# Causal attention with a routed feed-forward on one Trainium2 core: part of the softmax sums on ScalarE, the rest in one buffer on GpSimd

## The chip, the cores and the metric

The kernel runs on one core of a Trainium2 chip. The metric is the device time of one execution in microseconds: lower is better. Three runs of the kernel before stand beside one execution that was taken with the hardware profiler.

## The reference

Two sequences of 2048 positions with 512 features pass through one pre-norm block: attention with 16 heads of 32, rotary positions and a causal mask, then a feed-forward in which two of eight low-rank experts are chosen per position. All of it is fp32.

```python
x = x + attn(layernorm(x))
x = x + ffn(layernorm(x))

# attn: q, k, v = x @ Wq.T, x @ Wk.T, x @ Wv.T, split in 16 heads; q, k = rope(q), rope(k)
scores = einsum('bhqd,bhkd->bhqk', q, k) / sqrt(32)
attn = softmax(where(causal, scores, -inf))
return einsum('bhqk,bhkd->bhqd', attn, v) @ Wo.T      # heads put side by side again

# ffn: base layer, gate of two experts, low-rank update
result = x @ base_w.T + base_b
gate = top-2 of softmax(x @ router_w.T + router_b), made to add to 1
mid = einsum('nd,edr->ner', x, lora_A) * gate
return result + 2 * einsum('ner,erd->nd', mid, lora_B)
```

## The kernel before

**Blocks, steps and beats.** The 4096 positions are cut into eight blocks of 512 (`blocks`, four per sequence, j = 0 to 3 within a sequence). The 16 heads are taken four at a time, as the four 32-row quarters of a 128-row tile. So there are 32 steps (n, g): block n, group of heads g. A step needs its queries against the keys of all blocks up to its own: 4(j+1) key tiles of 128.

Every step has two passes over its scores, and the first pass of one step runs beside the second pass of the step before (`side_by_side`).

- `row_maxima`: the scores with queries in rows (`sm`, L367). VectorE takes the largest of each row into `pm`, with the causal mask on the diagonal block (L375) and without it elsewhere (L380). `split` writes the negated maxima as three bfloat16 parts into `parts`; `turned` transposes them (L397) into `max` (L401).
- `attend`: the scores with keys in rows (`sc`, L463). Two small bfloat16 matmuls per pair (`shift`, L471) add the negated maxima, ScalarE takes the exponential (`weigh`, L485) into a tile `pt` of four heads, GpSimd zeroes what lies above the diagonal (L494), and `weighted` multiplies the weights with the values into the bank `av` (L519).

In the inner loop of `side_by_side` two heads of the maxima go beside the other two of the weights; a tile of 128 keys or queries takes two such passes. `phase` counts them.

**Sums.** The softmax's denominators come out of the same weights. When two neighbouring key tiles have been weighted, GpSimd adds the second `pt` to the first (L534), and three phases later `summed` multiplies the sum with a column block of ones into the bank `den` (L545): one group of four matmuls for every two key tiles. After the last, the sums leave through DRAM to be spread over the partitions (`sums`, `few`), VectorE takes reciprocals, they come back (`over`, `sum`), and GpSimd multiplies `ctx` with them (L581).

**Other work.** `prepare` normalises and transposes the next block (`xnps_a`, L155) and projects keys, queries and values (L185, L210); `finish` makes the output projection (`ops`, L239), the router and the experts (`mid`, L265), and the base layer (`yps`, L320) of the block before, and stores it. They come as stages with a cost and a due phase in the list `waiting`; after every pass the main loop does what its running `credit` allows, and what is urgent.

**Order.** TensorE, ScalarE and VectorE run in the order in which the program is written (`manual_schedule`). The tile framework orders GpSimd and the DMA queue of SyncE itself. `between` runs what stands in `due`, the delayed `weighted` and `summed`; when a pass got nothing else, `ahead` may run a `summed` one phase early. `before` runs the `due` entries whose `pt` tile is about to be taken again, of which there are `PTS = 4`.

**Banks.** PSUM has eight banks. Six are handed out in turn by `bank` to scores, projections and transposes; `av` and `den` have one each.

```python
def bank(name, shape=(P, BLK), dtype=F32):
    banks[0] += 1
    return ps.tile(list(shape), dtype, tag=f"ps{banks[0] % 6}", name=name)
```

All weights are loaded once, at the start, and stay in SBUF.

Of the kernel before, what the change touches and what calls it, by code (L numbers as in the profile page):

```python
# [15 lines left out]
P = 128  # L16
# [13 lines left out]
PTS = 4  # L30
# [4 lines left out]
def preln_attention_moe_lora(  # L35
# [34 lines left out]
    def bank(name, shape=(P, BLK), dtype=F32):  # L70
        banks[0] += 1
        return ps.tile(list(shape), dtype, tag=f"ps{banks[0] % 6}", name=name)
# [54 lines left out]
    wo = load_weight(wo_t, "wo")  # L127
# [3 lines left out]
    base_w = load_weight(base_wt, "base_w")  # L131
    exp_out = const.tile([ER, D], F32, name="exp_out")
    nc.sync.dma_start(out=exp_out, in_=expert_out)

# [23 lines left out]
    def prepare(n):  # L158
# [23 lines left out]
        def project(which, w, g):  # L182
            pj = bank(f"{which}ps_{n}_{g}")
            for c in range(NC):
                nc.tensor.matmul(  # L185
                    out=pj,
                    lhsT=w[:, c, bass.ts(g, P)],
                    rhs=held["xn_t"][:, c, :],
                    start=(c == 0),
                    stop=(c == NC - 1),  # L190
                )
            if which == "k":
                dest = kv.tile([P, BLK], F32, tag="k", name=f"k_{n}_{g}")
            else:
                dest = wide.tile([P, BLK], F32, tag="q", bufs=3, name=f"q_{n}_{g}")
            made[which].append(dest)
            sw = p2.tile([P, BLK], F32, tag="tmp", bufs=5, name=f"sw_{which}_{n}_{g}")
            nc.vector.stream_shuffle(sw, pj, SWAP)  # L198
            nc.vector.tensor_mul(dest, pj, held["turn"][0])
            nc.gpsimd.tensor_mul(sw, sw, held["turn"][1])  # L200
            nc.gpsimd.tensor_add(dest, dest, sw)  # L201
# [25 lines left out]
    def finish(n, ctx_t):  # L227
# [4 lines left out]
        def load(t):  # L232
            held["x"].append(load_x(n, t, True))

        def output(t):
            xt = held["x"][t]
            po = bank(f"ops_{n}_{t}")
            for c in range(NC):
                nc.tensor.matmul(  # L239
                    out=po,  # L240
                    lhsT=ctx_t[c][:, bass.ts(t, P)],
                    rhs=wo[:, c, :],
                    start=(c == 0),
                    stop=(c == NC - 1),
                )
            nc.vector.tensor_add(xt, po, xt)
            held["by"].append(moments(xt, t, f"f{n}"))
# [68 lines left out]
        def result(t):  # L316
            xt = held["x"][t]
            po = bank(f"yps_{n}_{t}")
            for c in range(NC):
# [3 lines left out]
                    rhs=base_w[:, c, :],  # L323
# [22 lines left out]
    def row_maxima(s):  # L346
# [3 lines left out]
        j = blocks[n][1]  # L350
        pm = small.tile([P, NT, 4, NB], F32, tag="pm", name=f"pm_{n}_{g}")
        three = parts[(n * NC + g) % 2]
        spare = []

        def quad(c, *ts):
# [16 lines left out]
            def largest(r):  # L372
                for t, w, here in zip(ts, wide_of, some):
                    if c == j:
                        nc.vector.tensor_tensor_reduce(  # L375
                            sc[r][:, here], sc[r][:, here], mask[:, BLK - w :], 1.0,
                            3.0 * MASKED, ALU.add, ALU.max, pm[:, t, r, c : c + 1],
                        )
                    else:
                        nc.vector.reduce_max(pm[:, t, r, c : c + 1], sc[r], axis=AX.X)  # L380
                spare[:] = [sc[r]]

            return take, scores, largest

        def split():

            neg = spare[0][:, : NT * 4].rearrange("p (t r) -> p t r", t=NT)
            nc.vector.tensor_reduce(neg, pm[:, :, :, : j + 1], AX.X, ALU.max, negate=True)
            nc.vector.tensor_copy(three[:, :, :, 0], neg)
            nc.vector.tensor_sub(neg, neg, three[:, :, :, 0])  # L390
            nc.vector.tensor_copy(three[:, :, :, 1], neg)
            nc.vector.tensor_sub(three[:, :, :, 2], neg, three[:, :, :, 1])  # L392

        def turned():
# [6 lines left out]
            nc.scalar.copy(s["max"], tp.rearrange("p t q -> p (t q)"))  # L401

# [10 lines left out]
    def later(phases, tile, do, early=0):  # L413
        due.append((phase[0] + phases, tile, do, early))
        due.sort(key=lambda entry: entry[0])

    def between():
# [3 lines left out]
        for _ in range(many):  # L421
            due.pop(0)[2]()
        return many > 0

    def ahead():

        for i, entry in enumerate(due):
            if entry[0] - entry[3] <= phase[0]:
                return due.pop(i)[2]()


    def attend(s):
# [3 lines left out]
        diagonal = NT * j  # L436
# [3 lines left out]
        pts, index, paired = {}, {}, {}  # L440
# [10 lines left out]
        def quad(*kts):  # L451
# [24 lines left out]
            def weigh(r):  # L476
                if kts[0] not in pts:
                    pt = p2.tile(
                        [P, 4, BLK], F32, tag="pt", bufs=PTS, name=f"pt_{n}_{g}_{kts[0]}"
                    )  # L480
                    for kt in kts:
                        index[kt], pts[kt] = begun[0], pt
                    begun[0] += 1
                pt = pts[kts[0]]
                nc.scalar.activation(  # L485
                    pt[:, r, all_of], sc[r][:, all_of], AF.Exp, scale=1.0 / math.sqrt(DK)
                )
                if kts[0] >= diagonal and r % 2:
# [9 lines left out]
                    )  # L498

            def before():  # L500

                while any(tile <= begun[0] - PTS for _, tile, _, _ in due):
                    due.pop(0)[2]()

            def after():

                oldest = diagonal + 1 if kts[0] == tiles - 2 else kts[0] - kts[0] % 2
                later(2, index[oldest], lambda: weighted(kts))
# [3 lines left out]
        def weighted(kts):  # L512
            if kts[0] == 0:
                s["av"] = ps_o.tile([P, BLK], F32, tag="av", name=f"av_{n}_{g}")
            for kt in kts:
                jj, tt = divmod(kt, NT)
                for r in range(4):
                    rows = slice(DK * r, DK * r + DK)
                    nc.tensor.matmul(  # L519
                        out=s["av"][rows, low(kt) :],  # L520
                        lhsT=values[jj][g][:, tt, rows],
                        rhs=pts[kt][:, r, place(kt)],
                        start=(kt == 0),
                        stop=(kt == tiles - 2),
                    )

            for kt in kts:
                kt -= kt % 2
                paired[kt] = paired.get(kt, 0) + 1
                if paired[kt] == 2:  # L530
                    lo = low(kt + 1)
                    for r in (0, 2):
                        some = pts[kt][:, r : r + 2, place(kt, lo)]
                        nc.gpsimd.tensor_add(some, some, pts[kt + 1][:, r : r + 2, place(kt + 1)])  # L534
                    later(3, index[kt], lambda kt=kt: summed(kt), 1)
            if kts[-1] == tiles - 2:
                s["dest"] = wide.tile([P, BLK], F32, tag="ctx", bufs=6, name=f"ctx_{n}_{g}")
                nc.scalar.copy(s["dest"], s["av"])

        def summed(kt):  # L540
            lo = low(kt)
            if kt == 0:
                s["den"] = ps_o.tile([P, BLK], F32, tag="den", name=f"den_{n}_{g}")
            for r in range(4):
                nc.tensor.matmul(  # L545
                    out=s["den"][DK * r : DK * r + DK, lo:],
                    lhsT=ones,
                    rhs=pts[kt][:, r, lo:],
                    start=(kt == 0),
                    stop=(kt == tiles - 2),  # L550
                )
            if kt == tiles - 2:
                total = p2.tile([P, BLK], F32, tag="tmp", bufs=5, name=f"sum_{n}_{g}")
                nc.scalar.copy(total, s["den"])
# [36 lines left out]
    def side_by_side(maxima, weights):  # L591

        while len(maxima) > len(weights):
            take, scores, largest = maxima.pop(0)
            for do in (take, lambda r: scores(0, r), lambda r: scores(1, r), largest):
# [3 lines left out]
        for before, take, scores, shift, weigh, after in weights:  # L599
            before()  # L600
            if maxima:
                take_m, scores_m, largest = maxima.pop(0)
                for mine, other in (HALVES, HALVES[::-1]):
# [11 lines left out]
                    for o in other:  # L615
                        weigh(o)
                    if other == HALVES[0]:
# [17 lines left out]
    HALVES = ((0, 1), (2, 3))  # L635
    keys, values, queries, contexts = {}, {}, {}, {}
# [73 lines left out]
    for step in steps + [None]:  # L710
# [18 lines left out]
        for i in range(slots):  # L729
# [3 lines left out]
            for _ in side_by_side(*todo):  # L733
# [28 lines left out]
                if not given:  # L762
                    ahead()
# [7 lines left out]
    while due:  # L771
        due.pop(0)[2]()
# [55 lines left out]
```

## Time and profile before

| | us |
|---|---|
| median of three runs | 1983.7 |
| lowest and highest run | 1977.12, 1988.35 |
| profiled execution, its own time | 1982.82 |
| its span from first to last instruction | 1981.0 |
| TensorE busy | 1918.0 |
| VectorE busy | 1018.2 |
| GpSimd busy | 1008.7 |
| ScalarE busy | 768.0 |

The mean granted clock of TensorE was 0.987 of full speed. Line numbers (L367) are those of the kernel before unless the text says otherwise. A row of a group reads: line, engine, operation, tiles written and read, shapes, how many; busy time of the group in us and mean duration in ns; idle time of the engine just before them and what ended it. An fp32 matmul shows as two records. Records of matmuls that run side by side on parts of the array overlap, so groups of TensorE add to more than its busy time. A row of the timeline starts with the start and the length in us; PE is TensorE, PEld its weight loads, DVE VectorE, ACT ScalarE, POOL GpSimd.

### The profile page before, as it was taken

The page shows a single profiled execution, that of the slowest core. Times are in us where ns is not written, and L with a number is a line of the kernel's source. Part 1 is how long each engine was busy: PE and PEld are TensorE (multiplying, and loading weights), DVE is VectorE, ACT ScalarE, POOL GpSimd, SP SyncE. Part 2 cuts the span into 40 slices and gives each one's busy share as a digit, 9 for nine tenths or more (in the row PEclk, how much of TensorE's full clock was granted, in tenths as well). Part 3 has the DMA queues.
Part 4 walks back from the last instruction along what each step waited for, and adds up shares of the span by engine and source line. Part 5 has one row for each costly group of instructions (what it writes and reads, how often), then busy time and mean ns, then how long its engine had stood idle before and what let it go on. Part 6 is the DMA issues. An engine that isn't in the chain of part 4 may idle for free.

```text
span 1981.0 us, 31399 instructions
## 1 busy us (share of the span) xinstructions
PE 1918.0 (97%) x12256; PEld 731.2 (37%) x12256; DVE 1018.2 (51%) x2760; ACT 768.0 (39%) x1601; POOL 1008.7 (51%) x906
## 2 busy tenths in 40 slices
PE   7999999999999999999999999999999999999997
PEld 3433433333333333333343434333433333333333
DVE  3555555555554655553255546446565555555403
ACT  1323342344433444353532334224434334443451
POOL 3545554455464555355565345435555545553572
PEclk9999999999999999999999999989999999999999
DMA  5000110000100000100000001100011000001000
GB/s 186 23 12 13 32 35 22 7 7 28 60 1 7 7 1 18 48 23 8 10 28 12 28 28 38 49 7 7 2 38 49 1 6 7 1 7 44 6 7 22
DMA packets 34861, 46.33 MB, mean 23 GB/s; under 512 B 12956, under 2 KB 13468, under 8 KB 34712
## 3 DMA queue, kind: packets, MB, share of 16 engines
q1 hardware_dynamic: 34712, 44.32, 7.0%
q8 instruction: 96, 1.57, 0.3%
q14 instruction: 53, 0.43, 0.1%
HBM read 35.40 MB, written 8.90 MB: 22 GB/s over the span
## 4 chain that ended last, share of the span: by engine, by line
PE 83%; POOL 7%; issue 4%; DVE 4%; ACT 1%; DMA 1%; SPq 0%; POOLq 0%; DVEq 0%
PE sm L367 24%; PE av L519 13%; PE den L545 6%; PE ops L239 6%; PE vps L210 6%; PE qps L185 5%; PE kps L185 5%; PE yps L320 5%; PE sc L471 5%; PE sc L463 4%; POOL pt L534 3%; POOL pt L494 2%; PE mid L265 1%; PE yps L327 1%; ACT pt L485 1%
## 5 line engine op out<-in xcount | busy, mean ns | idle before, releaser
L485 ACT ACTIVATE pt<-sc 128x512 f32<-128x512 f32 (+1 forms) x1152 | 595.1, 572 | 950.8 <-PE sc L471 882.0
L534 POOL TENSOR_TENSOR pt<-pt,pt 128x1024 f32<-128x1024 f32 (+2 forms) x320 | 609.9, 1920 | 339.2 <-ACT pt L485 193.6
L463 PE MATMUL sc<-q,k 32*128 32x512 f32 (+3 forms) x2560 | 677.5, 576 | 10.7 <-DVE parts L392 10.1
L367 PE MATMUL sm<-k,q 32*128 32x512 f32 (+3 forms) x2560 | 644.1, 574 | 6.3 <-POOL q L201 3.6
L380 DVE TENSOR_REDUCE pm<-sm 128x1 f32<-128x512 f32 x768 | 490.8, 685 | 286.5 <-PE sm L367 273.6
L367 PEld LDWEIGHTS sm<-k,q 32*128 32x128 f32 x2560 | 221.4, 184 | 375.0 <-issue 148.7
L519 PE MATMUL av<-pt,v 128*32 128x512 f32 (+3 forms) x2560 | 306.0, 550 | 19.1 <-POOL pt L494 14.2
L375 DVE CUSTOM_DVE_ANT_0 sm<-sm,mask 128x128 f32<-128x128 f32 (+3 forms) x512 | 245.8, 512 | 141.8 <-PE sm L367 118.7
L471 PE MATMUL sc<-max,ones_b 3*128 3x512 bf16 (+3 forms) x1280 | 261.2, 346 | 0.0
L463 PEld LDWEIGHTS sc<-q,k 32*128 32x128 f32 x2560 | 233.1, 185 | 51.2 <-issue 24.2
L494 POOL TENSOR_SCALAR_AFFINE_SELECT pt<-pt 128x256 f32<-128x256 f32 (+1 forms) x192 | 93.0, 485 | 154.7 <-ACT pt L485 152.2
L545 PE MATMUL den<-pt,ones 128*32 128x512 f32 (+1 forms) x1280 | 163.3, 569 | 0.0
L519 PEld LDWEIGHTS av<-pt,v 128*32 128x32 f32 x2560 | 57.5, 109 | 201.5 <-issue 142.1
L185 PE MATMUL kps<-xnt_a,wk 128*128 128x512 f32 x256 | 123.3, 626 | 5.0 <-ACT xnt_a L156 4.9
L239 PE MATMUL ops<-wo,ctx 128*128 128x512 f32 x256 | 120.2, 614 | 2.7 <-POOL ctx L581 2.7
L320 PE MATMUL yps<-base_w,xnt_f 128*128 128x512 f32 x256 | 116.9, 599 | 2.6 <-DVE pm L380 1.6
L185 PE MATMUL qps<-xnt_a,wq 128*128 128x512 f32 x256 | 118.3, 605 | 0.0
L210 PE MATMUL vps<-wv,xnt_a 128*128 128x512 f32 x256 | 117.5, 604 | 0.0
L471 PEld LDWEIGHTS <-ones_b 3*128 3x128 bf16 x1280 | 78.3, 94 | 101.0 <-issue 94.5
L200 POOL TENSOR_TENSOR sw_q<-sw_q,sin 128x512 f32<-128x512 f32 x32 | 40.7, 1273 | 112.5 <-DVE sw_q L198 112.5
L200 POOL TENSOR_TENSOR sw_k<-sw_k,sin 128x512 f32<-128x512 f32 x32 | 40.7, 1273 | 109.2 <-DVE sw_k L198 93.8
L581 POOL TENSOR_TENSOR ctx<-ctx,sum 128x512 f32<-128x512 f32 x32 | 40.6, 1268 | 90.1 <-DMA sum<-over 84.8
(85 smaller groups left out, 1246.4 us busy)
## 6 DMA issues: line engine op xcount, KB each, us to landing
xa<-in_x SPq DMA_DIRECT2D x32, 256.0 KB
xf<-in_x SPq DMA_DIRECT2D x32, 256.0 KB
out<-xf SPq DMA_DIRECT2D x32, 256.0 KB
sum<-over SPq DMA_DIRECT2D x124, 64.0 KB
cos<-in_cos SPq DMA_DIRECT2D x8, 256.0 KB
sin<-in_sin SPq DMA_DIRECT2D x8, 256.0 KB
sums<-sum SPq DMA_DIRECT2D x124, 2.0 KB
wk<-in_wk_t SPq DMA_DIRECT2D x1, 1024.0 KB
```

Source lines behind the costliest of these rows:

```text
L185: nc.tensor.matmul(out=pj, lhsT=w[:, c, bass.ts(g, P)], rhs=held["xn_t"][:, c, :], start=(c == 0), stop=(c == NC - 1),)
L210: nc.tensor.matmul(out=pv, lhsT=held["xn_t"][:, c, bass.ts(t, P)], rhs=wv[:, c, :], start=(c == 0), stop=(c == NC - 1),)
L239: nc.tensor.matmul(out=po, lhsT=ctx_t[c][:, bass.ts(t, P)], rhs=wo[:, c, :], start=(c == 0), stop=(c == NC - 1),)
L367: nc.tensor.matmul(out=sc[r][:, some[i]], lhsT=q[rows, bass.ts(ts[i], P)], rhs=keys[c][rows, : wide_of[i]], start=True, stop=True,)
L375: nc.vector.tensor_tensor_reduce(sc[r][:, here], sc[r][:, here], mask[:, BLK - w :], 1.0, 3.0 * MASKED, ALU.add, ALU.max, pm[:, t, r, c : ...
L380: nc.vector.reduce_max(pm[:, t, r, c : c + 1], sc[r], axis=AX.X)
L463: nc.tensor.matmul(out=sc[r][:, place(kts[i])], lhsT=keys[jj][rows, bass.ts(tt, P)], rhs=q[rows, low(kts[i]) :], start=True, stop=False,)
L471: nc.tensor.matmul(out=sc[r][:, place(kts[i])], lhsT=ones_b[rows, :], rhs=s["max"][rows, low(kts[i]) :], start=False, stop=True,)
L485: nc.scalar.activation(pt[:, r, all_of], sc[r][:, all_of], AF.Exp, scale=1.0 / math.sqrt(DK))
L519: nc.tensor.matmul(out=s["av"][rows, low(kt) :], lhsT=values[jj][g][:, tt, rows], rhs=pts[kt][:, r, place(kt)], start=(kt == 0), stop=(kt ...
L534: nc.gpsimd.tensor_add(some, some, pts[kt + 1][:, r : r + 2, place(kt + 1)])
L545: nc.tensor.matmul(out=s["den"][DK * r : DK * r + DK, lo:], lhsT=ones, rhs=pts[kt][:, r, lo:], start=(kt == 0), stop=(kt == tiles - 2),)
```

## The change

- **Sums of whole blocks on ScalarE.** For `SUMMED[j]` leading key blocks of a step (0, 1, 2, 2 for j = 0 to 3) ScalarE takes exponentials of the `sm` tiles of the first pass, in place in PSUM, each row against the largest of its own key block (`pm`, now kept negated), and accumulates along the row into `se`. `split` then puts the distance between that maximum and the step's in `pm`; one small exponential makes factors of it, and VectorE adds up `se` times the factors into `part` (`brought_together`).
- **The remaining weights in one buffer.** The first key tile that is not summed in this way goes to a tile of a tag of its own (`acc`, two buffers); GpSimd adds every later `pt` to it, right after its exponential and mask. `pt` tiles become three.
- **One stretch of sums a step.** `summed` runs once per step, two phases after the last `weighted`: four matmuls of ones with the buffer, and 16 small ones that add `part`, in a bank from the ring.
- **Banks.** `den` has none of its own; seven banks go round.
- **`weighted` in halves.** When one entry is due and no planned work is urgent or due next, `between` runs only half of the 512 columns, and the rest after the next pass. `ahead` goes.
- **Weights.** `wo` and `base_w` are loaded for every block, in turn, into one buffer. The scale 1/sqrt(32) is multiplied into `wq` once, by ScalarE, at the first block's query projections.

```diff
-PTS = 4
+PTS = 3
...
-        return ps.tile(list(shape), dtype, tag=f"ps{banks[0] % 6}", name=name)
+        return ps.tile(list(shape), dtype, tag=f"ps{banks[0] % 7}", name=name)
...
+    def load_in_turn(src, name):
+        w = wide.tile([P, NC, D], F32, tag="w", name=name)
+        nc.sync.dma_start(out=w, in_=src.rearrange("(c p) o -> p c o", p=P))
+        return w
...
+            if n == 0 and which == "q":
+                some = wq[:, :, bass.ts(g, P)]
+                nc.scalar.activation(some, some, AF.Copy, scale=1.0 / math.sqrt(DK))
...
+            def exponentials(r):
+                if c < some_of:
+                    at = (slice(None), ts[0], r, slice(c, c + 1))
+                    nc.scalar.activation(
+                        sc[r], sc[r], AF.Exp, bias=pm[at], accum_out=s["se"][at]
+                    )
...
         def split():
-            nc.vector.tensor_reduce(neg, pm[:, :, :, : j + 1], AX.X, ALU.max, negate=True)
+            if j:
+                nc.vector.tensor_reduce(neg, pm[:, :, :, :j], AX.X, ALU.min)
+                nc.vector.scalar_tensor_tensor(neg, pd, -1.0, neg, ALU.mult, ALU.min)
+            else:
+                nc.vector.tensor_scalar(neg, pd, -1.0, None, ALU.mult)
...
+            if some_of:
+                nc.vector.tensor_sub(
+                    pm[:, :, :, :some_of],
+                    neg.unsqueeze(3).to_broadcast([P, NT, 4, some_of]),
+                    pm[:, :, :, :some_of],
+                )
...
+    def between():
+        many = sum(entry[0] <= phase[0] for entry in due)
+        many = min(many, 1 + many // 3)
+        spare = any(entry[2] <= phase[0] + 1 for entry in waiting)
+        if many == 1 and not spare:
+            due.pop(0)[2](1)
+        else:
+            for _ in range(many):
+                due.pop(0)[2](2)
...
+        def add():
+            while s["first"] and ready:
+                kt, r = ready.pop(0)
+                some = pts[summed_from][:, r : r + 2, low(kt) :]
+                nc.gpsimd.tensor_add(some, some, pts[kt][:, r : r + 2, place(kt)])
+
+        def summed(_):
+            den = bank(f"den_{n}_{g}")
+            for r in range(4):
+                nc.tensor.matmul(
+                    out=den[DK * r : DK * r + DK, :], lhsT=ones,
+                    rhs=pts[summed_from][:, r, :], start=True, stop=not SUMMED[j],
+                )
+            for t in range(NT if SUMMED[j] else 0):
+                for r in range(4):
+                    nc.tensor.matmul(
+                        out=den[DK * r : DK * r + DK, bass.ts(t, P)],
+                        lhsT=s["part"][:, t, r : r + 1].to_broadcast([P, DK]),
+                        rhs=ident, start=False, stop=t == NT - 1,
+                    )
...
                     for r in mine:
                         largest(r)
                     for o in other:
                         weigh(o)
+                    for r in mine:
+                        exponentials(r)
...
+    SUMMED = (0, 1, 2, 2)
```

## The prediction

> A beat, below, is one pass of the inner loop of `side_by_side`: two score matmuls of the maxima (`sm`, L367) and two of the weights (`sc`, L463), each on a quarter of the array, two shifts (L471), then whatever `between` and the planner append. Both kernels have 575 beats.
>
> **What bounds the kernel now.** First the page's busy time by engine, then the groups by line with shapes kept apart.
>
> ```profile
> PE 1918.0 (97%) x12256; PEld 731.2 (37%) x12256; DVE 1018.2 (51%) x2760; ACT 768.0 (39%) x1601; POOL 1008.7 (51%) x906
> ```
>
> TensorE bounds the kernel on average: it is idle for 63 of 1981.0 us. ScalarE has 1213 us free, but on average only.
>
> ```profile
> L485 ACT ACTIVATE pt<-sc 128x512 f32<-128x512 f32 x1024 | 553.2, 595 | 838.2 <-PE sc L471 802.0 <-PE sm L367 19.7 <-POOL pt L534 8.8
> ...
> L545 PE MATMUL den<-pt,ones 128*32 128x512 f32 x1024 | 143.0, 613 | 0.0
> ...
> L375 DVE DVE_READ_ACCUMULATOR2_ANT pm<- 128x1 f32 x512 | 72.7, 142 | 0.0
> ...
> L149 ACT ACTIVATE xa<-xa,mom_a 128x512 f32<-128x512 f32 x32 | 26.3, 820 | 1.8 <-POOL mom_a L145 1.3 <-DVE mom_a L142 0.5
> ```
>
> An fp32 matmul is two records, and four matmuls on different column quarters run together, so 1024 records are 128 full groups of `den`, and L545's 256 narrow records 32 more.
>
> Averages hide the order inside a beat, so third the timeline, over a stretch with no projections (several PE rows left out):
>
> ```profile
> 535.34 0.69 PE L367 MATMUL sm<-k,q 32*128 32x512 f32 x1
> ...
> 536.31 0.39 PE L471 MATMUL sc<-max,ones_b 3*128 3x512 bf16 x2
> 536.50 1.29 DVE L380 TENSOR_REDUCE pm<-sm 128x1 f32<-128x512 f32 x2 [1.00 <-PE sm L367]
> 536.63 1.06 PE L545 MATMUL den<-pt,ones 128*32 128x512 f32 x8
> 536.72 1.09 ACT L485 ACTIVATE pt<-sc 128x512 f32<-128x512 f32 x2 [1.14 <-PE sc L471]
> 537.62 0.69 PE L367 MATMUL sm<-k,q 32*128 32x512 f32 x1
> ```
>
> The beat takes 2.28 us: 0.97 for the scores, 0.32 for the shifts, 0.99 for one group of `den`. The beats before and after carry an `av` group (L519) there instead, at the same price. ScalarE begins 1.38 us after the beat does, and two exponentials take 1.09, so the second follows the first by 0.495.
>
> Fourth, a place where a matmul waits for its bank (VectorE rows, then weight loads, then matmuls, then ScalarE of the stretch from 881.5):
>
> ```profile
> 881.57 1.29 DVE L380 TENSOR_REDUCE pm<-sm 128x1 f32<-128x512 f32 x2 [1.58 <-PE sm L367]
> ```
> ```profile
> 882.91 0.18 PEld L463 LDWEIGHTS sc<-q,k 32*128 32x128 f32 x1 [0.18 <-DVE pm L380]
> ```
> ```profile
> 883.28 0.38 PE L471 MATMUL sc<-max,ones_b 3*128 3x512 bf16 x1
> 883.45 0.59 PE L463 MATMUL sc<-q,k 32*128 32x512 f32 x1
> 883.88 0.38 PE L471 MATMUL sc<-max,ones_b 3*128 3x512 bf16 x1
> ```
>
> VectorE lets the bank go at 882.86, the fourth score matmul of the beat starts 0.05 later, and its shift ends at 884.26, 1.35 after that start. Nothing behind it passes. The list of waits says that this is already common, though short:
>
> ```profile
> PEld sm L367 <- DVE pm L380: 144.9, 189, 0.8
> ```
>
> **What the change takes off TensorE.** `den` now: 128 full groups at 1.00 us and 32 of 256 columns at 0.57 (start to start in the timeline), 146 us. After: per step one full group, 32 x 1.00, and in the 24 steps with summed blocks four groups of 128 columns more (16 small matmuls with `part`). By the line through 1.00 and 0.57 a group of 128 takes 0.36; 24 x 4 x 0.36 = 34. Together 66: **-80 us**. In TensorE's instruction order of the changed kernel the 320 groups of `av` become 396, because 76 are cut in two; a cut costs 2 x 0.57 - 1.00 = 0.14: **+11 us**. The cutting also evens out the beats: one without a projection comes to 1.29 + 0.57 = 1.86 us. If nothing else held TensorE, that would be -69 us.
>
> **What it puts on ScalarE, and who waits for it.** 640 exponentials of `sm` tiles, in place in PSUM, with a bias from SBUF and an accumulator. In the program they stand behind the beat's two `weigh` exponentials, and the `sm` bank is free only when they end. No row shows this form. From below: L485's 0.595 us. From above: L149's 0.820 (two operands from SBUF, a source in SBUF) and the 0.142 of reading an accumulator on VectorE, 0.96. I take 0.595 + half of L149's surplus (one such operand of two, 0.11) + 0.06, by which VectorE's accumulator read outlasts its main instruction in the timeline (904.04 against 903.99): **0.77 us**, the row of L485 being the nearest in shape and source.
>
> The Trainium skill's page "ScalarE: Activation LUTs", section "What ACT_TABLE_LOAD costs", gives 93 ns for such an operand and nothing for the accumulator, which speaks against the change; by it the instruction would take 0.69 and the sum below would end at about +91 instead of +105. The same page, under "Step-by-step: what each stage is for", calls PSUM the faster destination without a figure, and no row here has ScalarE writing PSUM.
>
> Now the ring. A beat takes four banks (`sm`, `sc`, `sm`, `sc`) of seven. With no projection between, the fourth of the next beat is the first of this one: the `sc` matmul must wait until the first `sm` exponential has ended. Before, that bank was let go by a `weigh` or by VectorE. From a beat that started freely: 1.38 until `weigh` starts + 2 x 0.495 + 0.77 + 0.05 to the weight load, less 0.02 by which the fourth matmul trails the first: **3.17 us** a beat. From a beat that was itself held: 0.05 + 1.35 to the end of the late shift + 0.04 until ScalarE starts (881.76 to 881.80 in the timeline) + 0.495 + 0.77 = **2.70 us**. This is a chain through three queues; ScalarE's own work, 0.99 + 2 x 0.6 to 0.7, would allow 2.2 to 2.4.
>
> How many beats? In the instruction order of the changed kernel 284 beats have `weigh` and these exponentials both. Those with 3.2 us or more of TensorE's own work (98, mostly with a projection of 3.6 us) cover the chain. Walking the others in order: 88 follow a free beat and hold 2.17 us of work on average, 87 follow a held one and hold 1.87; the last 11 cover what is left of it. The floors cost 88 x (3.17 - 2.17) + 87 x (2.70 - 1.87) = **+160 us**. A further 18 beats have four `sm` tiles and no `sc`: four exponentials at some 0.70 are 2.8 us, 14 of them hold 1.5 to 2 us of work: **+14 us**.
>
> **The rest.** GpSimd: 320 adds become 256, and of the 1024-wide ones at 2.35 us 192 become 64; some 216 us less on an engine that did not bound, hidden under TensorE. They now form one serial stretch, and the diagonal masks (L494) queue behind it; `av` of the diagonal waits for those masks. Priced with the rivals. SyncE: `wo` and `base_w` are loaded once per block instead of once, 16 MB in place of 2, where 44 MB now fill 7% of the DMA engines. `base_w` waits for the block's last `ops` matmul, and the queue behind it (`sums`, `few`, `over` of a step) waits along; the `ctx` multiply behind those already waits 84.8 us on an idle engine, and the planner places output work well after it. On the tail, 10.1 us lie between the end of L239 (1949.65) and L320 (1959.61); the first 12.6 us of the run bring x and `wk`, 2 MB, so 1 MB fits. Uncovered it would cost 6 us a block. Scaling `wq`: four activations near 0.82, the first two beside the 5.2 us of the first key projection. `split`: two small VectorE operations more a step, near 0.2 us each, of which at most 6 us in all reach the shift. The scale left out of `weigh` and the negated maximum cost nothing: same operations on the same shapes. I set these at nothing and keep them in the range.
>
> **Sum.** -80 + 11 + 160 + 14 = +105 on the profiled execution's 1982.8 us, which is 0.9 below the median of 1983.7: **2088 us**. With 0.595 for the exponential the floors are 3.00 and 2.53 and the sum +75, 2058; with 0.96 they are 3.36 and 2.89 and the sum +139, 2122.
>
> **Rivals.** First, faster: the banks never hold TensorE, because ScalarE is ahead of what I read from two places in the timeline, and only its throughput counts. Then the light beats fall from 2.28 to 1.86 as written, and the heavy ones meet a floor of 0.99 + 2 x 0.605 = 2.2 us, which costs 43 us over the short ones: -69 + 43 = -26, 1957 us; with no floor at all 1914. It decides as soon as a heavy short beat averages under 2.3 us. For it: the average idle time of ScalarE. Against it: the waits on `pm`, which show that banks already hold TensorE, and a chain that exceeds 2.28 even with an exponential of 0.595.
>
> Second, slower still: GpSimd's stretch. In the eight steps of the last query blocks it adds four full key blocks in a row at 4.7 us each and then the diagonal, where two beats of 1.86 are 3.7. If masks and the closing sum are late by 5 us in each, that is 40 us on top: 2128.
>
> Third, nothing much: what the floors cost and what `den` frees cancel, 1974 to 1994. That would need an exponential far below 0.595 in most places, or projections spread evenly over the heavy beats.
>
> **Chances.** Forecast 0.68, GpSimd on top 0.11, faster 0.16, cancelled 0.05; the forecast's own range is 2040 to 2120. The range for 8 in 10 runs down to 1990 towards the other sign, and up to 2140 for the second rival. A measurement of this kernel tells about 0.5%, 10 us, from no change. Faster 0.16, same 0.04, slower 0.80.
>
> **What would show it.** Right: L405 (the new activation) near 0.77 us; weight loads of `sc` (L512) with long waits on ScalarE at L405; short beats of the second and third blocks near 2.7 and 3.2 us; light beats near 1.9; TensorE's busy share well under 97%. Wrong: L405 near 0.5 us of pitch with TensorE still at 97%, or waits that name GpSimd's adds (L603) or DMA ahead of L405.

## The result, and the profile after

The changed kernel took **2201.3 us** (four runs, 2198.7 to 2202.7) against 1983.6 for the kernel before on the same chip: a ratio of 1.110, with a 95% interval of 1.107 to 1.113. It is slower by 218 us where 105 were forecast. The profiled execution took 2202.0 us, its span is 2200.3.

First the busy time by engine of the changed kernel, and its row of granted clock in 40 slices (a digit is tenths of full speed):

```profile
PE 2073.1 (94%) x12608; PEld 809.2 (37%) x12608; DVE 1031.0 (47%) x2856; ACT 1197.6 (54%) x2909; POOL 790.2 (36%) x842
...
PEclk9899989899889899989989998999998999998989
```

The same row of the kernel before:

```profile
PEclk9999999999999999999999999989999999999999
```

TensorE's busy time rose by 155 us although matmuls were taken from it, for two reasons. The first is the clock: a matmul at a lower clock lasts longer. In the trace's clock record the clock is 1.0 or 0.5, and the stretches at 0.5 are whole multiples of 3.4 us (3.4 to 20.5; the end of the record cuts off the last). They sum to 52 us before and 296 after. If TensorE bounded all of them, the extra 244 us cost 122. The forecast had no term for this.

The second is that a score matmul that is held runs alone and not beside its neighbours. The widest group of `sc` matmuls, before and after:

```profile
L463 PE MATMUL sc<-q,k 32*128 32x512 f32 x1792 | 526.0, 644 | 0.0
L512 PE MATMUL sc<-q,k 32*128 32x512 f32 x1792 | 695.2, 681 | 7.2 <-ACT sm L405 6.9
```

One record lasts 37 ns longer, 6%, but the group is busy for 169 us longer, 32%. So part of the wait for a bank stands in TensorE's busy time, not in its idle time.

The groups of the exponential `weigh` and of the new activation, which is two records (busy time of the group, mean ns of one):

```profile
L535 ACT ACTIVATE pt<-sc 128x512 f32<-128x512 f32 x1024 | 554.2, 599 | 615.5 <-PE sc L520 589.6 <-PE sm L384 7.8 <-POOL pt L603 7.3
L405 ACT ACTIVATE sm<-sm,pm 128x512 f32<-128x512 f32 x640 | 427.1, 673 | 28.3 <-DVE pm L397 27.7
...
L405 ACT ACTIVATION_READ_ACCUMULATOR sm<-sm,pm 128x1 f32 x640 | 139.3, 218 | 0.0
```

By start times in the timeline (448.55 and 449.12 below) the second ends 0.79 us after the first began, and the next activation starts 0.66 after it: the two overlap.

Now a beat of the changed kernel that was held, in the timeline (rows of the other matmuls left out):

```profile
447.58 1.09 ACT L535 ACTIVATE pt<-sc 128x512 f32<-128x512 f32 x2 [0.55 <-PE sc L520]
...
448.55 0.67 ACT L405 ACTIVATE sm<-sm,pm 128x512 f32<-128x512 f32 x1
...
448.80 0.59 PE L384 MATMUL sm<-k,q 32*128 32x512 f32 x1
449.12 0.21 ACT L405 ACTIVATION_READ_ACCUMULATOR sm<-sm,pm 128x1 f32 x1
449.21 0.67 ACT L405 ACTIVATE sm<-sm,pm 128x512 f32<-128x512 f32 x1
449.39 0.18 PEld L512 LDWEIGHTS sc<-q,k 32*128 32x128 f32 x1 [0.83 <-ACT sm L405]
449.39 0.69 PE L512 MATMUL sc<-q,k 32*128 32x512 f32 x1
...
449.40 0.38 PE L520 MATMUL sc<-max,ones_b 3*128 3x512 bf16 x1
...
449.92 0.59 PE L512 MATMUL sc<-q,k 32*128 32x512 f32 x1
...
450.35 0.38 PE L520 MATMUL sc<-max,ones_b 3*128 3x512 bf16 x1
450.55 1.09 ACT L535 ACTIVATE pt<-sc 128x512 f32<-128x512 f32 x2 [0.55 <-PE sc L520]
```

Read it as a ring. ScalarE's `weigh` at 447.58 is followed by the exponential at 448.55; it and its accumulator read end at 449.34; 0.05 later the held `sc` matmul loads its weights; its second record ends at 450.51, and the next `weigh` starts at 450.55. From `weigh` to `weigh`: 2.97 us. The beat's other score matmuls had ended by 449.39, so the held one ran without them.

The list of waits (total us, times, longest us):

```profile
PEld sc L512 <- ACT sm L405: 117.6, 165, 1.6
POOL pt L603 <- PE av L578: 113.0, 7, 40.8
PEld av L578 <- POOL pt L542: 103.1, 59, 5.6
PE av L578 <- POOL pt L542: 67.7, 44, 5.3
```

The first is the wait that was forecast. The last two were 32.4 and 14.2 us before: `av` waits for GpSimd's diagonal masks. The timeline of such a diagonal (ScalarE, GpSimd and `av`):

```profile
571.38 1.08 ACT L535 ACTIVATE pt<-sc 128x512 f32<-128x512 f32 x2 [1.08 <-PE sc L520]
572.14 1.80 POOL L603 TENSOR_TENSOR pt<-pt,pt 128x768 f32<-128x768 f32 x1 [1.14 <-PE av L578]
...
573.89 0.64 POOL L542 TENSOR_SCALAR_AFFINE_SELECT pt<-pt 128x512 f32<-128x512 f32 x1
574.50 3.31 POOL L603 TENSOR_TENSOR pt<-pt,pt 128x256 f32<-128x256 f32 x3
...
574.59 0.85 PE L578 MATMUL av<-pt,v 128*32 128x384 f32 x8 [1.55 <-POOL pt L542]
```

The weights are there at 572.46, but GpSimd is in an addition until 573.94; the mask ends at 574.53, and TensorE has stood still for 1.55 us. What follows is in the table of windows (us of PE, PEld, DVE, ACT and POOL busy, each with its count of instructions; then granted clock, DMA share and GB/s):

```profile
570.00:573.00 3.00, 3.00 (x38) 1.88 (x32) 2.62 (x12) 1.41 (x4) 1.50 (x2) 1.00 0.81 298
573.00:575.50 2.50, 0.95 (x13) 0.29 (x14) 2.17 (x13) 0.63 (x2) 2.50 (x4) 0.99 0.44 102
575.50:579.00 3.50, 3.50 (x30) 1.73 (x32) 0.88 (x4) 1.38 (x4) 3.34 (x4) 0.50 0.22 84
579.00:583.00 4.00, 4.00 (x26) 1.24 (x19) 1.30 (x3) 2.42 (x6) 2.14 (x3) 0.50 0.00 0
```

One microsecond after the gap the clock is 0.50, with TensorE busy throughout, and it stays so until 595.9. Of the gaps in TensorE's work that are over 1.5 us and begin at full clock, the run without additions (below) has 6 and the changed kernel 21, 14.5 and 51.0 us in all; in 20 of the 21 the clock halves during the gap or within 2 us of its end.

### The profile page after: what moved, and what is told of

The parts are those of the page before. It is cut to its first block, busy times and chain, and to the rows that moved or that the text cites. A ratio compares the mean times of both kernels' runs of the same rounds, so it can differ in the third digit from the quotient of the medians.

```text
span 2200.3 us, 33913 instructions
## 1 busy us (share of the span) xinstructions
PE 2073.1 (94%) x12608; PEld 809.2 (37%) x12608; DVE 1031.0 (47%) x2856; ACT 1197.6 (54%) x2909; POOL 790.2 (36%) x842
## 3 DMA queue, kind: packets, MB, share of 16 engines
q8 instruction: 99, 1.62, 0.3%
## 4 chain that ended last, share of the span: by engine, by line
PE 78%; POOL 11%; issue 4%; ACT 4%; DVE 3%; DMA 0%; SPq 0%; ACTq 0%; POOLq 0%; DVEq 0%
PE sm L384 21%; PE av L578 11%; PE sc L512 9%; POOL pt L603 8%; PE qps L193 5%; PE ops L249 5%; PE vps L218 5%; PE kps L193 5%; PE yps L332 5%; PE sc L520 5%; POOL pt L542 2%; PE den L608 2%; ACT pt L535 2%; ACT sm L405 1%; PE yps L339 1%
## 5 line engine op out<-in xcount | busy, mean ns | idle before, releaser
L512 PE MATMUL sc<-q,k 32*128 32x512 f32 (+3 forms) x2560 | 856.5, 612 | 18.3 <-ACT sm L405 6.9
L384 PE MATMUL sm<-k,q 32*128 32x512 f32 (+3 forms) x2560 | 689.8, 618 | 12.9 <-ACT sm L405 5.3
L603 POOL TENSOR_TENSOR pt<-pt,pt 128x768 f32<-128x768 f32 (+3 forms) x256 | 392.0, 1537 | 155.0 <-PE av L578 113.0
L405 ACT ACTIVATE sm<-sm,pm 128x512 f32<-128x512 f32 x640 | 427.1, 673 | 28.3 <-DVE pm L397 27.7
L578 PE MATMUL av<-pt,v 128*32 128x512 f32 (+3 forms) x3168 | 339.2, 503 | 68.1 <-POOL pt L542 67.7
L512 PEld LDWEIGHTS sc<-q,k 32*128 32x128 f32 x2560 | 285.5, 197 | 160.7 <-ACT sm L405 117.6
L520 PE MATMUL sc<-max,ones_b 3*128 3x512 bf16 (+3 forms) x1280 | 325.8, 364 | 0.0
L578 PEld LDWEIGHTS av<-pt,v 128*32 128x32 f32 x3168 | 70.3, 113 | 312.0 <-issue 188.1
L648 POOL TENSOR_TENSOR ctx<-ctx,sum 128x512 f32<-128x512 f32 x32 | 40.6, 1269 | 319.8 <-DMA sum<-over 272.1
L405 ACT ACTIVATION_READ_ACCUMULATOR sm<-sm,pm 128x1 f32 x640 | 139.3, 218 | 0.0
L520 PEld LDWEIGHTS <-ones_b 3*128 3x128 bf16 x1280 | 93.7, 98 | 108.4 <-issue 102.4
L208 POOL TENSOR_TENSOR sw_k<-sw_k,sin 128x512 f32<-128x512 f32 x32 | 40.8, 1273 | 257.9 <-DVE sw_k L206 243.2
```

Source lines behind the costliest of these rows:

```text
L384: nc.tensor.matmul(out=sc[r][:, some[i]], lhsT=q[rows, bass.ts(ts[i], P)], rhs=keys[c][rows, : wide_of[i]], start=True, stop=True,)
L405: nc.scalar.activation(sc[r], sc[r], AF.Exp, bias=pm[at], accum_out=s["se"][at])
L512: nc.tensor.matmul(out=sc[r][:, place(kts[i])], lhsT=keys[jj][rows, bass.ts(tt, P)], rhs=q[rows, low(kts[i]) :], start=True, stop=False,)
L520: nc.tensor.matmul(out=sc[r][:, place(kts[i])], lhsT=ones_b[rows, :], rhs=s["max"][rows, low(kts[i]) :], start=False, stop=True,)
L578: nc.tensor.matmul(out=s["av"][rows, lo:hi], lhsT=values[jj][g][:, tt, rows], rhs=pts[kt][:, r, at + lo : at + hi], start=(kt == 0 and lo ...
L603: nc.gpsimd.tensor_add(some, some, pts[kt][:, r : r + 2, place(kt)])
```

## The experiments

Every edit is to the changed kernel unless it says otherwise. Differences are between medians on the same chip, to the kernel before. The time at half clock is that of the profiled execution.

**The two halves of the change, each taken out.**

```diff
# no_exp
-                    nc.scalar.activation(
-                        sc[r], sc[r], AF.Exp, bias=pm[at], accum_out=s["se"][at]
-                    )
+                    pass        # and in row_maxima: nc.vector.memset(s["se"], 1.0)
# no_adds
-                nc.gpsimd.tensor_add(some, some, pts[kt][:, r : r + 2, place(kt)])
# neither: both edits
```

Without the exponentials:

> The changed kernel without the 640 exponentials on ScalarE (the accumulated sums are set to a constant, so the sums of whole blocks are left out). Ring theory (the exponentials hold the bank that the next beat's fourth matmul needs): all heavy short beats fall from 3.1 us to about 1.9, the time goes to 1915 to 1970 us, and the granted clock comes back to 0.98. GpSimd theory (masks queue behind the adds, TensorE idles and loses its clock): the waits of av on the masks stay near 68 us and the time stays above 2080 us.

Without the additions:

> The changed kernel without the 256 adds on GpSimd (the remaining weights are left out of the sums). Ring theory: light beats lose their waits on the masks, but heavy short beats stay at 3.1 us: 2100 to 2160 us, clock at most 0.96. GpSimd theory: below 2060 us and the clock near 0.98.

Without either:

> The changed kernel without the exponentials and without the adds, so TensorE's part of the change alone. Both theories: the -69 us of the sum are there, 1905 to 1930 us, clock 0.98 or more. If it is above 1950 us, a third cost lies in the order, the seven banks or the loads of weights.

| | us | to before | half clock, us |
|---|---|---|---|
| neither | 1867.9 | -114 | 70 |
| additions alone (no_exp) | 1976.1 | -6 | 180 |
| exponentials alone (no_adds) | 2098.6 | +117 | 169 |
| both (the change) | 2201.3 | +218 | 296 |

The parts nearly add: the exponentials cost 231 us alone and 223 beside the additions, the additions 108 alone and 101 beside the exponentials, and TensorE's relief is 114. Without the exponentials and without the additions the times lie 6 us above and 1 us below the ranges of the ring theory, and outside those of the other; with neither, 37 us below the range that both expected. The profiled executions of "neither" and of "exponentials alone" were the slowest of their four, 14 and 16 us above the median, at a mean clock of 0.982 and 0.960 where the others had 0.990 to 0.992 and 0.970 to 0.971. So a typical execution of these two has less half clock than the table, some 35 and 125 us (an estimate: twice the missing share of the clock times the span).

The run with neither shows TensorE still full:

```profile
PE 1826.7 (97%) x12608; PEld 744.0 (40%) x12608; DVE 1027.4 (55%) x2880; ACT 773.5 (41%) x1629; POOL 403.7 (21%) x586
```

**Two rings of banks** (2146.6 us, +165): the `sm` tiles get four banks of their own, so that an exponential no longer holds up an `sc` matmul (passes without `sm` tiles take from both rings).

```diff
-        return ps.tile(list(shape), dtype, tag=f"ps{banks[0] % 7}", name=name)
+        tag = f"pm{banks[0] % 4}" if ring == 0 else f"ps{banks[1] % 3}"
+        return ps.tile(list(shape), dtype, tag=tag, name=name)
```

> The whole changed kernel, with the seven banks in two rings: four for the tiles of the maxima, three for everything else, so that a matmul of the weights never waits for an exponential of the maxima. Ring theory: heavy short beats fall from 3.1 us to 2.4 to 2.6, ScalarE's own pace, 160 beats x 0.6 = 100 us, and part of the lost clock comes back: 2020 to 2100 us. GpSimd theory: 2170 to 2200 us.

I lined up 525 of the 575 beats with the written order and compared each with TensorE's own work at the prediction's prices. Short heavy beats (under 2.75 us of own work, with `weigh` and the exponentials) average 3.09 us at full clock in the changed kernel and 2.30 here; with those at half clock their time beyond own work falls by 131 us. So the ring was their bound. But the long heavy beats, where projections share the other three banks, rise by 45, and half clock stays at 245 us: 53 us come back; the time lies between the ranges of the two theories.

**The masks moved to VectorE** (2230.4 us, +251), to free them from GpSimd's queue, by a product with a triangle of ones; and without any additions (2150.0 us, +167):

```diff
-                    nc.gpsimd.affine_select(...)
+                    for k in range(len(kts)):
+                        some = on[:, :, bass.ts(k, P)]
+                        nc.vector.tensor_mul(some, some, keep.unsqueeze(1).to_broadcast([P, 2, P]))
```

> The whole changed kernel, but the causal zeros of the weights are made by VectorE (a product with a triangle of ones and zeros) instead of GpSimd, so no av matmul waits behind GpSimd's adds. Theory that the masks queue behind the adds: av waits for GpSimd no more, most of the 103 us that leaving out the adds gave come back, 2100 to 2145 us. Theory that the adds themselves hold the kernel (weights tiles come free late, the closing sum waits): above 2170 us.

> No additions at all, and the diagonal masks as VectorE products (256 x 0.77 us in the earlier run with masks on VectorE). It gives the price of the masks' new place by itself. If the masks behind the additions were the cost of the additions and their new place costs as much again, this comes 90 to 130 us above the run without additions (2099), 2190 to 2230. If the place on VectorE is free, it stays at 2095 to 2105, and the additions cost their 130 us by holding the pt tiles, whatever the masks do.

The cure failed. The first time lies in the range of the theory that the additions themselves hold the kernel, but it can't decide: the second, which met neither of its ranges, shows that the new place has a price of its own. Without additions the masks' new place costs 50 us by itself (2150 against 2099); the additions, put back, cost another 84. The group and the waits of the run with both show why:

```profile
L548 DVE TENSOR_TENSOR pt<-pt,keep 128x256 f32<-128x256 f32 x256 | 191.8, 771 | 30.4 <-ACT pt L541 29.6
```
```profile
POOL pt L607 <- DVE pt L548: 91.7, 54, 13.8
```

VectorE pays 192 us for what GpSimd did in 93, and now the additions wait for the masks.

**Combinations**: rings and masks on VectorE (2163.4 us, +184); the same with one summed block fewer, `SUMMED = (0, 1, 1, 1)` (2146.1, +166); masks on VectorE, one ring, and no block summed on ScalarE, `SUMMED = (0, 0, 0, 0)` (2057.7, +78).

> Two rings of banks (4 and 3) and VectorE's masks together. If the two costs are separate, the gains add: 2201 - 54 - 60 to 100 = 2050 to 2085 us. If the slow clock is what both share, more than the sum: below 2040 us, with a granted clock above 0.97.

> As the one before, with SUMMED = (0, 1, 1, 1): 384 exponentials in place of 640 and 448 adds on GpSimd in place of 256. Ring theory: 256 exponentials fewer, each worth 0.15 to 0.36 us, 40 to 90 us less than the kernel with 640, 1960 to 2030 us. If GpSimd's adds bound it instead (4.7 us for a whole tile against two beats of some 1.9 without a projection), no gain or a loss.

> SUMMED = (0, 0, 0, 0) with VectorE's masks and one ring of seven: no exponentials of the maxima, every weights tile is added by GpSimd (about 1130 us of adds, 1500 us busy in all). Ring theory alone: near the 1868 us of the kernel with neither exponentials nor adds, at most 1920 us. If GpSimd's stretch holds TensorE through the three weights tiles, 1950 to 2100 us, with ScalarE's weigh waiting for GpSimd.

The first two missed their ranges, by 78 and 116 us; the third lies in the range given for GpSimd's stretch. Fewer exponentials help each time (17 and 173 us), but what they no longer sum goes to GpSimd, and half clock is 319 us in the last.

**Which additions.** Leaving out those of key tiles before the diagonal (2184.7 us, +202) or those of diagonal tiles (2107.6 us, +125):

```diff
-                    ready.extend((kt, r - 1) for kt in kts)
+                    ready.extend((kt, r - 1) for kt in kts if kt >= diagonal)   # or: < diagonal
```

> Leaves out the 64 GpSimd additions of whole key tiles (1024 wide, before the diagonal), so the denominators lack them; the 192 additions of diagonal tiles stay. Theory A (the whole-tile additions start late, because the first of them waits for the first av, and the diagonal masks queue behind them in GpSimd's order): nearly all of the 103 us that all additions cost goes with these 64, so about 2110 to 2130 us and hardly any wait of av for L542. Theory B (the additions between the masks on the diagonal itself delay the next mask): most of the cost stays, 2170 to 2195 us. If the two share it by their busy time, 64 x 2 x 2.35 / 2 = 150 us against 240, about 2160.

> Leaves out the 192 GpSimd additions of diagonal tiles and keeps the 64 of whole key tiles. Theory A: the cost stays, 2170 to 2195 us, with waits of av for L542 as long as in the changed kernel (longest 5 us). Theory B: 2110 to 2130 us.

The expectations miscounted: the first leaves out 48 and the second 208. The diagonal's additions carry 93 us, the others 16. Theory B holds (2107.6 is 2 us below its range); the long waits for the first `av` (up to 40.8 us) hardly matter.

**No masks at all** (the causal zeroes are left out, the additions stay; 2123.2 us, +142), and **the diagonal's additions shared** between GpSimd and VectorE (2168.3 us, +187):

```diff
-                if kts[0] >= diagonal and r % 2:
+                if False:
# shared: emitted after the tile's av
+                on = nc.vector if r and kt >= diagonal else nc.gpsimd
+                on.tensor_add(some, some, pts[kt][:, r : r + 2, place(kt)])
```

> Leaves out the 192 causal masks of GpSimd (L542); the additions stay. If TensorE pays for the diagonal additions because the masks, and behind them av, are late, nearly all of the 103 us goes: 2095 to 2115 us, with the half-clock time down to that of the run without additions (169 us). If it pays through pt tiles that come free late or through the closing sum, the time stays at 2175 to 2200.

> The whole computation: of the additions of diagonal tiles, two heads on GpSimd and the other two on VectorE, after the tile's av. If GpSimd's throughput on the diagonal is the cost, half of its additions there leave and most of the 94 us comes back: 2115 to 2150 us. If VectorE is as full there (as with the masks moved to it), 2170 to 2220.

Without masks 76 of the 101 us go (8 us short of the expected range), half clock falls to 158 us and the gaps over 1.5 us from 21 to 9. Leaving out the masks also takes 93 us of work from GpSimd; but with the additions left out and the masks kept, `av` on TensorE waits 5.6 us for masks, and in the changed kernel 67.7. So the wait of `av` for a mask behind an addition is the main path; what the other 25 us are is open. The clock row without masks:

```profile
PEclk9999999999899999999999999999998999997989
```

Sharing gave back 31 us, a third of what the diagonal's additions cost; the time lies just below the second range. The edit also moves all additions behind their tile's `av`, and no run parts the two. The wait for the masks fell from 103.1 to 38.5 us:

```profile
PEld av L575 <- POOL pt L542: 38.5, 33, 5.6
```

and VectorE's part is not cheap (1.30 us for 768 elements; GpSimd's 1.81 became 1.92, and its masks of 256 elements went from 0.41 to 0.53). What keeps the rest was not settled.

**The accumulator** (2167.4 us, +186):

```diff
-                        sc[r], sc[r], AF.Exp, bias=pm[at], accum_out=s["se"][at]
+                        sc[r], sc[r], AF.Exp, bias=pm[at]      # se filled with 1.0
```

> The 640 exponentials without their accumulator output (se is filled once a step with a constant). L405 then ends about 0.11 us sooner (0.673 instead of 0.79 with its accumulator read). By the chain 175 short heavy beats lose 0.11 each, 19 us, and a little half-clock time with them: 2165 to 2185 us. If the accumulator read also keeps ScalarE from overlapping the next instruction, the second exponential of a beat starts sooner as well and some 40 to 60 us go: 2140 to 2165.

```profile
L406 ACT ACTIVATE sm<-sm,pm 128x512 f32<-128x512 f32 x640 | 398.8, 673 | 28.3 <-DVE pm L398 27.8
```

The main record is as long as before, 673 ns, and short heavy beats fall from 3.09 to 2.98, by the 0.11 that the read outlasts it. The total falls by 33 us (20 to 47 by the interval of the ratio), within the first range.

**The kernel before without its own 320 additions** (1976.1 us, -6; half of the weights are missing from its denominators):

> The kernel before without its 320 GpSimd additions (its denominators lack half of the weights); den keeps its 160 groups. If the forecast's -69 us for TensorE was right and the remaining 45 of the 114 are what GpSimd's additions already cost in the kernel before, this comes to 1935 to 1945 us. If the additions before were hidden, it stays at 1975 to 1985, and the relief of TensorE was mis-sized by 45 us.

Its additions were hidden. The busy times of this kernel:

```profile
PE 1910.7 (97%) x12256; PEld 731.1 (37%) x12256; DVE 1018.1 (52%) x2760; ACT 767.7 (39%) x1601; POOL 403.9 (21%) x586
```

600 us less work on GpSimd, for 6 us. So the relief of 114 us does not come from GpSimd's additions.

**A candidate** that computes everything, with no exponentials of `sm` tiles and the additions of all tiles shared between GpSimd and VectorE, masks on GpSimd (2005.5 us, +23; ratio 1.010, 1.008 to 1.013):

```diff
-    SUMMED = (0, 1, 2, 2)
+    SUMMED = (0, 0, 0, 0)
...
+                on = nc.vector if r else nc.gpsimd      # additions emitted after the tile's av, as above
```

> A candidate that computes everything: no exponentials of sm tiles (no key block summed on ScalarE), masks on GpSimd, all later weights added into the one buffer, two heads on GpSimd and the other two on VectorE, each after its tile's av. From the run with neither exponentials nor additions, 1868, less the 34 us of small den matmuls, 1834; if both engines hide their share, some 60 us of late masks and tiles remain: 1890 to 1930, clearly below the kernel before (1984). If VectorE's additions (about 210 x 0.6 to 1.2 us) hold up its row maxima and so the banks, or GpSimd and VectorE slow each other, 2000 to 2060.

```profile
PE 1905.7 (95%) x11840; PEld 745.6 (37%) x11840; DVE 1370.0 (69%) x3072; ACT 770.1 (39%) x1605; POOL 1074.5 (54%) x874
```

It is the best of the whole computations tried, in the second range of its expectation, and does not beat the kernel before. Half clock is 206 us, and an addition of 1024 elements took 1.62 us on VectorE and 2.50 on GpSimd, where GpSimd alone took 2.35.

## Why the prediction was right or wrong

The direction was right and the size wrong: 113 us short. The runs split the miss: the additions +101, the exponentials +57, TensorE's relief -45.

**TensorE's relief, -69: mis-sized; it measured -114.** The two profiled executions are only 101 us apart, because the one with neither half was above its median. Counted from the start of each TensorE record to the start of the next, which adds up to the span, `den` fell from 152.2 to 52.9 us, -99 where -80 was taken; `av` rose by 5 where +11 was. The price of a lone full group was right: 119 of 120 such groups at full clock take 1.00 us from start to start. The step that failed is the price of what closes a step. In the run with neither:

```profile
446.39 1.07 PE L603 MATMUL den<-pt,ones 128*32 128x512 f32 x8
447.27 1.06 PE L609 MATMUL den<-ident,part 128*32 128x128 f32 x32
448.25 0.69 PE L385 MATMUL sm<-k,q 32*128 32x512 f32 x1
```

The full group takes 0.88, and the four groups of 128 columns that follow it take 0.98 together, 0.25 each and not the 0.36 of the line through 1.00 and 0.57, which a lone `av` group of that width does take. Over the run the two are 53 us where 66 were taken. In the same run the waits of the `sm` weight loads for banks on VectorE fell from 183 to 47 us, but the score matmuls with their shifts take 809.6 us from start to start, and 809.7 before: shorter waits for banks freed nothing. The 6 us by which `den` before exceeds the 146 taken, and some 7 in small groups, were not resolved.

**The exponential, 0.77 us: right in its sum.** It ended 0.79 after its start. Its two surcharges were off in opposite ways, which is luck: 0.11 was taken for the bias operand and 0.06 for the accumulator, and the runs show 0.07 and 0.11. The main record is 673 - 599 = 74 ns longer than that of `weigh`, which has no such operand but writes to SBUF and not to PSUM; no run parts the two. The Trainium skill's page "ScalarE: Activation LUTs", section "What ACT_TABLE_LOAD costs", states 93 for the operand. For the accumulator, on which the page says nothing of time, the runs show the 0.11 that its read ends later.

**The chain from a free beat, 3.17: right** (median 3.17 over those beats). **From a held beat, 2.70: wrong, 2.97.** The step that failed is that only the second `weigh` waits for the late shift. In the timeline the first shift is done at 449.78, and yet the first `weigh` starts at 450.55, when the held `sc` matmul, issued ahead of that shift, has ended too. So both exponentials stand behind it: 0.05 + 1.12 + 0.04 + 0.97 + 0.79. It is not a single case: in 121 of the 153 such holds at full clock, the first `weigh` starts 0.04 or 0.05 us after the held matmul's end. Over 87 beats that is 24 us.

**The floors, +160 and +14: near, by luck in part.** From neither to the exponentials alone, the short heavy beats' time beyond own work rose from 17 to 191 us, so 174 for 160, with part of it half clock. Long heavy beats, which were to cover the chain, rose by 33. The remaining 24 of the 231 lie outside the beats I could line up; the +14 was not measured by itself.

**GpSimd: the step that failed most.** "An engine that did not bound, hidden under TensorE" was read from its average, 51%, which indeed fell to 36%. But its additions and masks meet on the diagonal. The additions there take 279 us (392 less 48 x 2.35), 8.7 us a step, and the masks 2.9: 11.6 us in some six short beats. The second rival named this mechanism, at 0.11 and +40, for eight of the 32 steps. In these eight TensorE stood still for masks for 37.4 us, close to its price; the other 30.3 of the 67.7 are spread over the other steps, and the rival counted late masks alone. The cost was 101.

Between the profiled executions without additions and with them (2114.3 and 2202.0 us), TensorE's idle time grew by 58 us and its busy time by 30, while half clock grew by 127 us. So TensorE standing still is two thirds of the difference. That the lower clock is the rest fits, but no run parts it.

**The clock: missing.** The Trainium skill's page "TensorE: Matmul & The Clock Gate", section "What's actually happening", has the clock halve after an idle window of some 3.4 us. The stretches here have that grain, but one gap of 1.55 us was enough, and in the run without additions 13 of the 20 stretches have no gap over 0.8 us in the 6 us ahead of them. All stretches of a run begin on one grid of 3.4 us. Cut into the windows of this grid, the changed kernel has 435 at full clock in which TensorE is busy for 97.5% or more, and none of them is followed by half clock; of the 85 in which it is busy for less than 90%, 34 are. In the kernel before these are 0 of 482 and 11 of 53. So idle time well short of a window goes ahead of half clock here; what spared the other 51 of the 85 is open. The section "A second HAM failure mode: psum-queue depth-cycling" of that page, which tells of short idles that set the clock going up and down, is nearer to these runs.

**The rivals.** The faster one fell: the ring held TensorE exactly where it was looked for, and the two rings took that away. The cancelled one fell with it. The list of waits of the changed kernel has no wait for `wo` or `base_w`, and `den`'s weight loads wait 1.1 us in all for the last addition: setting these at nothing held. GpSimd's wait for `sum` on its way through DRAM rose from 84.8 to 272.1 us, but in the run without additions it is 301.5, so it is not what the additions cost.

## What to carry to other kernels

Price an engine in the stretch where its work meets, not by its share: GpSimd's load fell by a fifth, and its new place cost 101 us. When a change adds short stalls to a TensorE that is nearly full, look at the clock too: here 58 us of added idle time came with 127 us more at half clock. Look into the busy time as well, which can hide a wait: matmuls that used to run side by side and now run one after the other count as busy all the while. And follow a bank through all its users: one more reader between two matmuls makes a ring whose length, not ScalarE's load, sets the beat.

## What the runs showed of the hardware

A matmul that was issued late held back the report of a later, shorter one: the consumer of the shift that was done at 449.78 started at 450.55, with the end of the earlier matmul at 450.51 (the ends of matmuls are modelled by the profile), and 121 of 153 such holds are alike. The clock was halved in stretches of 3.4 us and stayed down while TensorE was 100% busy, for 20 us at 575.5. Four groups of four narrow matmuls (128 columns) in a row took 0.98 us, a lone one 0.36. An accumulating activation of 512 elements is two records, 673 and 218 ns, which overlap to 0.79 us, and the next one starts 0.66 us after it.
